# The end of a two-layer decoder on one core: grouped stores, one rare condition, four PSUM banks and spread row scaling

## The chip, the core and the metric

The kernel runs on one core of a Trainium2 chip. A core has five engines that run their own instruction streams: TensorE (PE, with its weight loads PEld), VectorE (DVE), ScalarE (ACT), GpSimd (POOL) and SyncE (SP, which mostly issues DMAs). They wait for each other on semaphores. The metric is the device time of one execution in microseconds (us), as the median of several runs; lower is better.

## The reference, cut to what matters

The reference is a decoder of two layers on x of 8 x 256 tokens with 256 features, in float32. Each layer adds self attention, cross attention to a context, and a feed-forward part, each on a layer norm of x. The change touches only the last part, the feed-forward of the second layer: a shared expert for every token, and one of eight routed experts for each token (top 1), weighted by a sigmoid gate.

```python
scores_aE = x_aD @ router_DE
vals_aK, idx_aK = jax.lax.top_k(scores_aE, K)                   # K = 1
masked_aE = jnp.full_like(scores_aE, -jnp.inf).at[jnp.arange(a)[:, None], idx_aK].set(vals_aK)
gates_Ea = jax.nn.sigmoid(masked_aE).T
routed_in_EaD = jax.lax.stop_gradient(gates_Ea[:, :, None] * x_aD[None, :, :])
mid_EaF = jax.nn.silu(jnp.einsum('ead,edf->eaf', routed_in_EaD, w1_eDF)) * jnp.einsum('ead,edf->eaf', routed_in_EaD, w3_eDF)
routed_out_EaD = jnp.einsum('eaf,efd->ead', mid_EaF, w2_eFD)
shared_aD = jax.nn.silu(x_aD @ ws1_DF) * (x_aD @ ws3_DF) @ ws2_FD
out_aD = shared_aD + routed_out_EaD.sum(axis=0)
...
x = x + _L1_ffn_ref(_layernorm(x, axis=-1), L1_ffn_router_DE, ...)
```

There are a = 2048 tokens, D = 256 features, F = 704 hidden features and 8 experts.

## The kernel before

Tokens are held as 16 tiles of 128 x 256 in `x`, on 128 partitions. All but the feed-forward part of the second layer is untouched by the change. That part is `token_experts`, and it has two kinds of work.

The shared expert works in four quarters of 512 tokens. `quarter(q)` makes the hidden values: six chunks of the 704 features (five of 128 and one of 64). For each chunk TensorE makes two products of 512 columns, h1 and h3 (L864; tiles `h1` and `h3` have two PSUM banks each), ScalarE takes silu of h1 into `sl` (L856), and VectorE multiplies `sl` by h3 into `mid` (L857). `joined(q, mid, i)` then makes the second product for one tile of 128 tokens (`out`, L1209, in a bank of the PSUM pool `emm`, which has two) and adds it to `x` on VectorE (L1220). The hidden values of quarters 0 and 1 are made before `token_experts` starts, under the names `hx` and `slx`.

The routed experts need tokens that are sorted by expert. VectorE works out each token's place `pos_i`. `gated(j)` scales the rows of token tile j: one product of the row's inverse deviation and its gate (L1234) and one normalisation into `xg` (L177). `put_rows(j)` scatters these rows on GpSimd's queue into `xs` in DRAM (an indirect DMA, L1294). Then `slots` works through 17 tiles of sorted rows. For each it reads the rows (GpSimd's queue, L1343; each read waits until all sixteen scatters have landed), reads an expert's weights (SyncE's queue, from `packs`; `w13` and `w2` have four buffers each), turns the rows on TensorE (`xrp`, L1370, in a bank of `emm`), makes the two products, and stores the result `ye` from ScalarE's queue. At the end sixteen indirect DMAs (L1446) gather each token's result back into `xg`.

The order of the stage is written by hand for TensorE and VectorE. It is: the second products of quarter 0 among the routing arithmetic, with the scaling of tiles 0 to 3 and their scatters; the scaling of tiles 4 to 15, each followed by its scatter on GpSimd; quarter 2; the second products of quarters 1 and 2; the 17 tiles; quarter 3; the gathers; and the last loop. In that loop VectorE adds four gathered tiles (L1456), each of them but 12 to 15 is stored by SyncE (L1458), then `joined(3, mid, i)` finishes tile 12 + i, which is stored too (L1460). These are sixteen stores of 128 KB each.

After the loop come two rare cases, which the inputs do not meet. Where the sorted tokens fill more than 17 tiles, the rest is worked off (`more`, a register load and a branch on every engine, L1464 and L1465). Where the first layer's routing was odd (`odd`, a load and a branch, L64 and L65), a whole second program `general` runs.

Of the kernel before, what the change touches and what calls it, by code (L numbers as in the profile page):

```python
# [28 lines left out]
F32 = mybir.dt.float32  # L29
BF16 = mybir.dt.bfloat16  # L30
I32 = mybir.dt.int32
U32 = mybir.dt.uint32
AF = mybir.ActivationFunctionType
ALU = mybir.AluOpType
# [4 lines left out]
P = 128  # L39
# [11 lines left out]
SLOTS = NT + E - 1  # L51
FIRST = 2 * FF
TILES = NT + E // 2
PAIRED = NT - E // 2
NEG = -1.0e30


@with_exitstack
def decoder(ctx: ExitStack, tc: tile.TileContext, a: dict, out: bass.AP):
    nc = tc.nc  # L60
    keep = ctx.enter_context(tc.tile_pool(name="keep", bufs=1))
    odd_i = keep.tile([P, 1], I32, name="odd_i")
    plain(tc, a, out, odd_i)
    odd = nc.values_load(odd_i[0:1, 0:1], min_val=0, max_val=1)  # L64
    with tc.If(odd > 0):  # L65
        general(tc, a, out)


@with_exitstack
def plain(ctx: ExitStack, tc: tile.TileContext, a: dict, out: bass.AP, odd_i: bass.AP):  # L70

    nc = tc.nc

    const = ctx.enter_context(tc.tile_pool(name="const", bufs=1))
    small = ctx.enter_context(tc.tile_pool(name="small", bufs=4))
    dram = ctx.enter_context(tc.tile_pool(name="dram", bufs=1, space=DRAM))

# [58 lines left out]

    dens = const.tile([P, 3, NT, H], F32, name="dens")

    xs = dram.tile([TILES * P, D], F32, name="xs")
    ye = dram.tile([TILES * P, D], F32, name="ys")

    yo = dram.tile([(TILES - 16) * P, D], F32, name="yo")

    packs = dram.tile([E, P, 2 * FIRST + NFC * D], F32, name="packs")

    def pack(e):

# [364 lines left out]
    def expert_tables():  # L514
        nc.sync.dma_start(gate, a["L0_ffn_gate_w"].rearrange("(c p) e -> p c e", p=P))
        nc.gpsimd.dma_start(experts, a["L0_ffn_experts"].rearrange("e (c p) f -> p e c f", p=P))
        zero = one.tile([P, D], F32, name="zero")
        nc.gpsimd.memset(zero, 0.0)
        nc.gpsimd.dma_start(xs.rearrange("(s p) d -> p s d", p=P), zero.unsqueeze(1).to_broadcast([P, TILES, D]))
        nc.gpsimd.dma_start(  # L520
            ye[17 * P :].rearrange("(s p) d -> p s d", p=P), zero.unsqueeze(1).to_broadcast([P, TILES - 17, D])
        )
        nc.gpsimd.dma_start(yo.rearrange("(s p) d -> p s d", p=P), zero.unsqueeze(1).to_broadcast([P, TILES - 16, D]))
        for e in range(E):
            nc.gpsimd.dma_start(packs[e, FF % P :, 2 * FIRST + FF // P * D :], zero[FF % P :])

        key_i = one.tile([P, E, TOP], I32, name="key_i")
        nc.gpsimd.iota(key_i, [[1, E], [E, TOP]], base=0, channel_multiplier=0)
        key = one.tile([P, S], F32, name="key")
        nc.vector.tensor_copy(key, key_i.rearrange("p e r -> p (e r)"))  # L530
        kps = mm.tile([P, 2, 2 * P], F32, tag="mm", name="kps")
        keycol = one.tile([P, 2], F32, name="keycol")
        for h in range(2):
            nc.tensor.transpose(kps[:, h, :P], key[:, bass.ts(h, P)], ident)
        nc.vector.tensor_copy(keycol, kps[:, :, 0])
        for h in range(2):
            nc.vector.tensor_scalar(later[:, h, :], key, keycol[:, h : h + 1], None, ALU.is_gt)
        num_i = one.tile([P, S], I32, name="num_i")
        nc.gpsimd.iota(num_i, [[1, S]], base=0, channel_multiplier=0)
        nc.vector.tensor_copy(num, num_i)  # L540
# [649 lines left out]
    def token_experts(phase):  # L1190
        one = phase.enter_context(tc.tile_pool(name="e1", bufs=1))
        work = phase.enter_context(tc.tile_pool(name="e2", bufs=2))
        wts = phase.enter_context(tc.tile_pool(name="e3", bufs=4))
        mm = phase.enter_context(tc.tile_pool(name="emm", bufs=2, space=PSUM))
        hp = phase.enter_context(tc.tile_pool(name="eh", bufs=2, space=PSUM))
        ws2, mid_s = shared["ws2"], shared["mid_s"]

# [34 lines left out]
        def gated(j):  # L1232
            (mv, rs), t = norms[j // 2], j % 2
            nc.vector.tensor_tensor(rs[:, t : t + 1], rs[:, t : t + 1], gates[:, j : j + 1], ALU.mult)  # L1234
            normed(xg[:, j, :], x[:, j, :], mv, rs, t)
# [51 lines left out]
        nc.vector.tensor_tensor(place, place, route["hot"], ALU.mult)  # L1287
        pos = one.tile([P, NT], F32, name="pos")
        nc.vector.tensor_reduce(pos, place, AX.X, ALU.add)
        pos_i = one.tile([P, NT], I32, name="pos_i")  # L1290
        nc.vector.tensor_scalar(pos_i, pos, TILES * P - 1.0, None, ALU.min)

        def put_rows(j):
# [25 lines left out]
        exp_f = one.tile([P, n_at], F32, name="exp_f")  # L1319
        nc.vector.tensor_reduce(exp_f, past.rearrange("p n k e -> p n (k e)"), AX.X, ALU.add)  # L1320
        nc.vector.tensor_scalar(tcol, tcol, filled[:, 0:1], None, ALU.is_ge)
        exp_i = one.tile([P, n_at], I32, name="exp_i")
        nc.vector.scalar_tensor_tensor(exp_i, tcol, 1.0 - E, exp_f, ALU.mult, ALU.add)
        gated(3)
        joined(0, mids[0], 3)
        put_rows(3)
        for j in range(4, NT):
            gated(j)
            put_rows(j)
        filled_i = one.tile([P, 1], I32, name="filled_i")  # L1330
        nc.vector.tensor_tensor(filled[:, 1:2], full_at[:, E:], all_at[:, E:], ALU.add)
        nc.vector.tensor_copy(filled_i, filled[:, 1:2])
        nc.vector.tensor_copy(odd_i, route["odd"])
        mids.append(quarter(2)[0])
        for i in range(4):
            joined(1, mids[1], i)
        for i in range(3):
# [50 lines left out]
        def outof(t, mid, sets):  # L1388
            ps = mm.tile([P, 2 * D], F32, tag="mm", name="out")[:, :D]
            for i in range(NFC):  # L1390
                for k, h in enumerate((slice(0, 64), slice(64, P))):
                    nc.tensor.matmul(  # L1392
                        ps[h],
                        mid[:, i, h],
                        sets[k % len(sets)][1][:, i, :],
                        start=i == 0,
                        stop=i == NFC - 1,
                        skip_group_check=True,
                    )
            yr = work.tile([P, D], F32, tag="yr", name="yr")  # L1400
            nc.scalar.copy(yr, ps)
            nc.scalar.dma_start(ye[bass.ts(t, P), :] if t < 17 else yo[bass.ts(t - 16, P), :], yr)

        def slots(order, beside=None):

            n = len(order)
            xr = [rows(t) for t in order[:2]]
            sets = [first_weights(order[0])]  # L1410
            if n > 1:
                sets.append(first_weights(order[1]))
            second_weights(sets[0])
            xrT = turned(xr)
            if beside:
                beside()
            xr = [rows(t) for t in order[2:4]]
            ahead = into(sets[0], xrT[0])
            for i, t in enumerate(order):
                now = ahead  # L1420
                if i + 2 < n:
                    sets.append(first_weights(order[i + 2]))
                if i + 1 < n:
                    second_weights(sets[i + 1])
                if i + 2 < n and i % 2 == 0:
                    xrT += turned(xr)
                    xr = [rows(t) for t in order[i + 4 : i + 6]]
                if i + 1 < n:
                    ahead = into(sets[i + 1], xrT[i + 1])
                outof(t, now, sets[i])  # L1430
# [14 lines left out]
        for j in places:  # L1445
# [4 lines left out]
                in_offset=bass.IndirectOffsetOnAxis(ap=pos_i[:, j : j + 1], axis=0),  # L1450
            )

        with tc.issue_after(last.ins), tc.manual_schedule(engines={mybir.EngineType.DVE}):
            for i in range(4):
                for j in places[4 * i : 4 * i + 4]:
                    nc.vector.tensor_tensor(x[:, j, :], x[:, j, :], xg[:, j, :], ALU.add)  # L1456
                    if j < 12:
                        nc.sync.dma_start(ov[j], x[:, j, :])  # L1458
                joined(3, mid, i)
                nc.sync.dma_start(ov[12 + i], x[:, 12 + i, :])  # L1460

        more = nc.values_load(filled_i[0:1, 0:1], min_val=2 * NT, max_val=2 * TILES - 1)  # L1464
        with tc.If(more > 34):  # L1465
            with tc.manual_schedule(engines={mybir.EngineType.PE}):
                slots([17])
                with tc.If(more > 36):
                    slots([18, 19])
            nc.vector.tensor_copy(pos, pos_i)  # L1470
            nc.vector.tensor_scalar(pos, pos, -16.0 * P, 0.0, ALU.add, ALU.max)
            beyond = one.tile([P, NT], I32, name="beyond")
            nc.vector.tensor_copy(beyond, pos)
            for j in range(NT):
                nc.gpsimd.indirect_dma_start(
                    out=xg[:, j, :],
                    out_offset=None,
                    in_=yo[:, :],
                    in_offset=bass.IndirectOffsetOnAxis(ap=beyond[:, j : j + 1], axis=0),
                )  # L1480
                nc.vector.tensor_tensor(x[:, j, :], x[:, j, :], xg[:, j, :], ALU.add)
                nc.sync.dma_start(ov[j], x[:, j, :])

    with ExitStack() as phase:
        token_experts(phase)
    w_s.close()


@with_exitstack
# [934 lines left out]
```

## Time and profile before

| what | value |
|---|---|
| median of three runs | 1406.7 us (1406.29 to 1408.69) |
| profiled execution | 1409.21 us |
| its span, first to last instruction | 1407.5 us |
| mean granted TensorE clock | 0.992 |
| TensorE busy | 1357.9 us, 96% of the span |
| VectorE, ScalarE, GpSimd busy | 36%, 32%, 28% |
| chain of work that ended last | PE 81%, DVE 6%, DMA 6% |

The profile shows one execution, so its times are summed against its own span; 1.7 us lie around the span. A row of the timeline gives the start, the length, the engine, the line of the kernel, the operation, the tile written and the tiles read, the shapes and how many instructions are taken together; in square brackets stands the idle time of the engine before it, and what ended it ("issue" means that the profile shows no releaser). PEclk is the clock that TensorE was granted, 1.00 for full speed. SPq, POOLq and so on are the engines' sequencers, which issue DMAs and take branches. Stage by stage, the last 240 us are: from 1171 to 1184 us second products and routing, from 1184 to 1206 us row scaling, scatters and quarter 2, to 1227 us second products, to about 1355 us the 17 tiles, then quarter 3 from 1363 us, and the last loop from 1382 us.

### The profile page before, as it was taken

Reading aid. Unit: us, or ns where it says so; the run is one execution under the profiler, and the core shown is the slowest. Engines: PE = TensorE matmul, PEld = TensorE weight load, DVE = VectorE, ACT = ScalarE, POOL = GpSimd, SP = SyncE. Lnnn points to the kernel's source line nnn. Section 1 sums busy time; section 2 is a strip of 40 time slices with the busy share of each in tenths; the row PEclk is TensorE's granted clock in tenths of the full one; section 3 lists DMA queues with packets and bytes.
Section 4 is the critical chain, followed back from the end, with each engine's and each line's share of the span. In section 5 each row is a group of like instructions: output and inputs, shape, how many; then the busy total and the mean of one; then the engine's idle time right before and its main releaser. Section 6 shows DMA issues by size and latency. Waiting matters only on the chain.

```text
span 1407.5 us, 28704 instructions
## 1 busy us (share of the span) xinstructions
PE 1357.9 (96%) x12198; PEld 884.4 (63%) x12198; DVE 502.7 (36%) x1465; ACT 456.8 (32%) x730; POOL 394.8 (28%) x499
## 2 busy tenths in 40 slices
PE   6999999999999999999999999999999999999995
PEld 3666756756766666665565656565565645788873
DVE  5443553653655744420122313221211336222212
ACT  2555444444444344422221313132221311122220
POOL 4232142142043244212141414233241523200013
PEclk9999999999999999999999999999999999999998
DMA  9950000000000006010101011010101013499943
GB/s 320 342 193 17 16 17 8 17 16 1 2 9 2 4 7 219 1 63 16 31 16 46 11 37 31 16 32 16 31 1 32 1 31 117 175 377 401 394 142 109
DMA packets 47069, 116.62 MB, mean 83 GB/s; under 512 B 8416, under 2 KB 30544, under 8 KB 42576
## 3 DMA queue, kind: packets, MB, share of 16 engines
q1 hardware_dynamic: 39056, 92.74, 19.3%
q0 software_dynamic: 5152, 18.89, 3.6%
q10 hardware_dynamic: 2720, 3.02, 0.6%
q8 instruction: 100, 1.64, 0.5%
q14 instruction: 41, 0.34, 0.1%
HBM read 104.00 MB, written 27.93 MB: 94 GB/s over the span
## 4 chain that ended last, share of the span: by engine, by line
PE 81%; DVE 6%; DMA 6%; POOL 3%; issue 2%; ACT 1%; SPq 1%; ACTq 0%; DVEq 0%; POOLq 0%
PE fm L191 12%; PE st L249 8%; PE o L281 8%; PE vps L191 8%; PE h L191 6%; PE wo L191 4%; PE ox L1055 4%; PE stx L1017 4%; PE out L1392 3%; PE qk L191 2%; PE hx L864 2%; PE tr L198 2%; PE out L1209 2%; PE h L864 2%; DMA packs<-L_ffn_w_eDF 2%; PE den L1031 2%
## 5 line engine op out<-in xcount | busy, mean ns | idle before, releaser
L281 PE MATMUL o<-pT,padv 128*64 128x256 f32 (+1 forms) x1536 | 171.6, 365 | 1.2 <-POOL pT L261 1.2
L258 ACT ACTIVATE pT<-st 128x1024 f32<-128x1024 f32 (+1 forms) x128 | 110.4, 915 | 88.3 <-PE st L249 87.5
L281 PEld LDWEIGHTS o<-pT,padv 128*64 128x64 f32 x1536 | 103.1, 137 | 53.0 <-issue 10.3
L249 PE MATMUL st<-qm,kT 64*128 64x256 f32 (+1 forms) x1024 | 116.2, 365 | 1.0 <-DVE qm L227 0.6
L191 PE MATMUL fm<-ctxT,wkv_x 128*64 128x256 f32 x1024 | 112.9, 380 | 0.0
L191 PE MATMUL vps<-wkv_x,ctxT 128*64 128x512 f32 x512 | 111.8, 593 | 0.0
L249 PEld LDWEIGHTS st<-qm,kT 64*128 64x128 f32 x1024 | 89.2, 188 | 25.9 <-issue 15.6
L191 PEld LDWEIGHTS fm<-ctxT,wkv_x 128*64 128x64 f32 x1024 | 73.1, 137 | 37.3 <-issue 1.3
L1023 POOL TENSOR_TENSOR both<-pTx 128x512 f32<-128x512 f32 x64 | 79.6, 1272 | 57.5 <-ACT pTx L1021 33.9
L1021 ACT ACTIVATE pTx<-stx 128x1024 f32<-128x1024 f32 x64 | 62.0, 1021 | 89.9 <-PE stx L1017 86.8
L191 PE MATMUL h<-xrT,w 128*64 128x128 f32 (+1 forms) x1936 | 86.9, 250 | 1.5 <-issue 1.5
L191 PEld LDWEIGHTS h<-xrT,w 128*64 128x64 f32 x1936 | 84.3, 137 | 4.4 <-issue 2.0
L191 PEld LDWEIGHTS vps<-wkv_x,ctxT 128*64 128x64 f32 x512 | 36.5, 137 | 68.9 <-issue 68.6
L258 ACT ACTIVATE pT<-st,kbias 128x1024 f32<-128x1024 f32 x64 | 68.0, 1113 | 28.8 <-PE st L249 28.7
L173 POOL TENSOR_TENSOR lnrs<-lnve,mhalf 128x2 f32<-128x2 f32 x48 | 34.2, 717 | 146.9 <-DVE lnve L171 93.7
L249 PE MATMUL st<-qm,memk 64*128 64x256 f32 x512 | 68.8, 393 | 0.5
L856 ACT ACTIVATE sl<-h 128x128 f32<-128x128 f32 (+1 forms) x114 | 35.3, 310 | 100.7 <-PE h L191 57.1
L1017 PE MATMUL stx<-qTx,kTx 64*128 64x256 f32 x512 | 64.3, 391 | 2.5 <-ACT pTx L1021 2.5
L857 DVE TENSOR_TENSOR midr<-sl,h 128x128 f32<-128x128 f32 x102 | 29.4, 288 | 101.5 <-PE h L191 69.7
L168 DVE BATCH_NORM_STATS2 lxst<-yx 128x6 f32<-128x256 f32 x16 | 6.0, 419 | 162.4 <-ACT yx L1115 162.4
L191 PE MATMUL qk<-l_wqkv,xnT 128*64 128x512 f32 x256 | 62.2, 608 | 0.7 <-ACT xnT L201 0.7
L261 POOL TENSOR_SCALAR_AFFINE_SELECT pT<-pT 128x512 f32<-128x512 f32 x64 | 39.5, 638 | 83.0 <-ACT pT L258 79.8
(272 smaller groups left out, 2082.5 us busy)
## 6 DMA issues: line engine op xcount, KB each, us to landing
w<-packs SPq DMA_DIRECT2D x22, 1408.0 KB
w<-packs SPq DMA_DIRECT2D x22, 768.0 KB
rs<-rd SPq DMA_DIRECT2D x16, 512.0 KB
packs<-L_ffn_w_eDF SPq DMA_DIRECT2D x8, 704.0 KB
packs<-L_ffn_w_eDF SPq DMA_DIRECT2D x8, 640.0 KB
packs<-L_ffn_w_eFD SPq DMA_DIRECT2D x8, 640.0 KB
ctxT<-ctx_T SPq DMA_DIRECT2D x8, 512.0 KB
wkv_x<-L_xattn_Wkv POOLq DMA_DIRECT2D x1, 4096.0 KB
```

The lines of the kernel that those rows point to most:

```text
L191: nc.tensor.matmul(out[h], lhsT[:, h], rhs, start=start, stop=stop, skip_group_check=True)
L249: nc.tensor.matmul(st[:, g, i, :n], kT[rows, c, bass.ts(kt, P)], qm[rows, 2 * mq + i, c, q0:], start=True, stop=True,)
L258: nc.scalar.activation(pT[:, :, :, :n], st[:, :, :, :n], AF.Exp, scale=scale, **kb)
L261: nc.gpsimd.affine_select(out=pT[:, :, :, :P], in_=pT[:, :, :, :P], compare_op=ALU.is_ge, fill=0.0, base=0, pattern=[[0, 2], [0, 2], [1, P ...
L281: nc.tensor.matmul(o[64 * i : 64 * i + 64, mq, q0:], v_pad[:, kt, 4 * c + 2 * mq + i, 2 * g : 2 * g + 2, :], pTs[kt][:, g, i, : S - q0], s ...
L856: nc.scalar.activation(sl, h1, AF.Silu)
L864: nc.tensor.matmul(h, shared["ws13"][:, c, lo : lo + P], shared["xnT"][:, c, bass.ts(q, 2 * S)], start=c == 0, stop=c == 1)
L1017: nc.tensor.matmul(st[:, g, kt, :], kT[rows, c, bass.ts(kt, P)], qT[rows, c, :], start=True, stop=True)
L1021: nc.scalar.activation(pT, st, AF.Exp, scale=scale)
L1023: nc.gpsimd.tensor_tensor(both, pT[:, :, 0, :], pT[:, :, 1, :], ALU.add)
L1055: nc.tensor.matmul(o[XD * g : XD * (g + 1), i, :], v[:, kt, 2 * (c2 + i) + g, :], pT[:, g, kt, :], start=kt == 0, stop=kt == 1, skip_group ...
L1392: nc.tensor.matmul(ps[h], mid[:, i, h], sets[k % len(sets)][1][:, i, :], start=i == 0, stop=i == NFC - 1, skip_group_check=True,)
```

## The change

There are four edits.

1. The last loop stores the four tiles of a group with one DMA of 512 KB where it stored each of them with its own. Tiles 12 to 15 are still stored singly. There are 7 stores instead of 16.
2. The two rare cases stand under one condition. VectorE works out `rare_i` (is the number of filled tiles above 17, plus `odd`) before quarter 2, and one load and one branch on it follow the last stores. The code for more than 17 tiles becomes a function `beyond` of its own. For this `pos_i`, `exp_i`, `filled_i` and `rare_i` move to the outermost SBUF pool, and the DRAM tensors `xs`, `packs` and `yo` to an outer DRAM pool.
3. The PSUM pool `emm` has four banks instead of two.
4. The scaling and scattering of tiles 4 to 15 is written two tiles at a time after each of the six chunks of quarter 2.

```diff
+COMMON = NT + 1
...
-    odd_i = keep.tile([P, 1], I32, name="odd_i")
-    plain(tc, a, out, odd_i)
-    odd = nc.values_load(odd_i[0:1, 0:1], min_val=0, max_val=1)
-    with tc.If(odd > 0):
-        general(tc, a, out)
+    dram = ctx.enter_context(tc.tile_pool(name="dram", bufs=1, space=DRAM))
+    odd_i, filled_i, rare_i = (keep.tile([P, 1], I32, name=n) for n in ("odd_i", "filled_i", "rare_i"))
+    pos_i = keep.tile([P, NT], I32, name="pos_i")
+    exp_i = keep.tile([P, PAIRED + 2 * (TILES - PAIRED)], I32, name="exp_i")
+    xs = dram.tile([TILES * P, D], F32, name="xs")
+    packs = dram.tile([E, P, 2 * FIRST + NFC * D], F32, name="packs")
+    yo = dram.tile([(TILES - COMMON + 1) * P, D], F32, name="yo")
+    stored = plain(tc, a, out, dram, odd_i, filled_i, rare_i, pos_i, exp_i, xs, packs, yo)
+    rare = nc.values_load(rare_i[0:1, 0:1], min_val=0, max_val=2)
+    with tc.If(rare > 0):
+        filled = nc.values_load(filled_i[0:1, 0:1], min_val=2 * NT, max_val=2 * TILES - 1)
+        with tc.If(filled > 2 * COMMON):
+            beyond(tc, out, pos_i, exp_i, xs, packs, yo, stored)
+        odd = nc.values_load(odd_i[0:1, 0:1], min_val=0, max_val=1)
+        with tc.If(odd > 0):
+            general(tc, a, out)
...
-        mm = phase.enter_context(tc.tile_pool(name="emm", bufs=2, space=PSUM))
+        mm = phase.enter_context(tc.tile_pool(name="emm", bufs=4, space=PSUM))
...
-        for j in range(4, NT):
-            gated(j)
-            put_rows(j)
-        filled_i = one.tile([P, 1], I32, name="filled_i")
         nc.vector.tensor_tensor(filled[:, 1:2], full_at[:, E:], all_at[:, E:], ALU.add)
         nc.vector.tensor_copy(filled_i, filled[:, 1:2])
         nc.vector.tensor_copy(odd_i, route["odd"])
-        mids.append(quarter(2)[0])
+        nc.vector.tensor_scalar(filled[:, 1:2], filled[:, 1:2], 2 * COMMON + 0.5, None, ALU.is_gt)
+        nc.vector.tensor_tensor(rare_i, filled[:, 1:2], route["odd"], ALU.add)
+        mids.append(mid_s[0])
+        for i, _ in enumerate(hidden_shared(2, pair, silu)):
+            for j in (2 * i + 4, 2 * i + 5):
+                gated(j)
+                put_rows(j)
...
+        stored = []
         with tc.issue_after(last.ins), tc.manual_schedule(engines={mybir.EngineType.DVE}):
             for i in range(4):
-                for j in places[4 * i : 4 * i + 4]:
+                group = places[4 * i : 4 * i + 4]
+                for j in group:
                     nc.vector.tensor_tensor(x[:, j, :], x[:, j, :], xg[:, j, :], ALU.add)
-                    if j < 12:
-                        nc.sync.dma_start(ov[j], x[:, j, :])
+                if i:
+                    lo = group[0]
+                    stored.append(nc.sync.dma_start(ov[lo : lo + 4].rearrange("t p d -> p t d"), x[:, lo : lo + 4, :]))
                 joined(3, mid, i)
-                nc.sync.dma_start(ov[12 + i], x[:, 12 + i, :])
-        more = nc.values_load(filled_i[0:1, 0:1], min_val=2 * NT, max_val=2 * TILES - 1)
-        with tc.If(more > 34):
...
+                stored.append(nc.sync.dma_start(ov[12 + i], x[:, 12 + i, :]))
+        return stored
```

## The prediction

> **What bounds the kernel now.** I read the page first (busy shares, chain), then the windows of the last 250 us, then TensorE's timeline there, then every engine's timeline from 1380 us on, and last SyncE's waits and branches.
>
> ```profile
> PE 1357.9 (96%) x12198; PEld 884.4 (63%) x12198; DVE 502.7 (36%) x1465; ACT 456.8 (32%) x730; POOL 394.8 (28%) x499
> ...
> PE 81%; DVE 6%; DMA 6%; POOL 3%; issue 2%; ACT 1%; SPq 1%; ACTq 0%; DVEq 0%; POOLq 0%
> ```
>
> TensorE (PE) is the bound over the whole span; the edits can only pay where it has a hole, or after its last product. The windows show both places.
>
> ```profile
> 1188.00:1192.00 4.00, 2.69 (x7) 0.90 (x5) 3.78 (x13) 0.00 (x0) 3.09 (x4) 1.00 0.98 380
> 1192.00:1196.00 4.00, 2.38 (x3) 1.17 (x4) 2.09 (x8) 0.60 (x1) 2.89 (x4) 0.65 1.00 404
> ...
> 1224.00:1340.00 116.00, 113.79 (x2031) 99.23 (x2030) 25.47 (x88) 32.78 (x108) 6.92 (x13) 1.00 0.93 366
> ...
> 1380.00:1400.00 20.00, 12.83 (x54) 9.69 (x52) 8.27 (x22) 0.59 (x1) 5.42 (x5) 0.95 0.44 137
> 1400.00:1407.50 7.50, 0.00 (x0) 0.00 (x0) 0.00 (x0) 0.00 (x0) 0.00 (x0) 0.50 0.13 41
> ```
>
> The columns are length, busy time of PE, PEld, DVE, ACT, POOL, then granted clock, DMA share, GB/s. At 1188 to 1196 PE is busy 5.07 of 8 us, with the clock at 0.65 in the second half, while DVE is nearly full. From 1400 on no engine computes for 7.5 us.
>
> ```profile
> 1170.99 8.02 PE L1209 MATMUL out<-ws,mid 128*128 128x256 f32 x36
> 1179.25 2.86 PE L1209 MATMUL out<-ws,mid 128*128 128x256 f32 x12 [0.24 <-DVE x L1220]
> 1181.94 8.75 PE L864 MATMUL h<-xnTe,ws 128*128 128x512 f32 x20
> 1193.62 12.05 PE L864 MATMUL h<-xnTe,ws 128*128 128x512 f32 x24 [2.93 <-issue]
> 1205.51 18.29 PE L1209 MATMUL out<-ws,mid 128*128 128x256 f32 x84
> ```
>
> The third and fourth rows are quarter 2. It stops after two and a half chunks for 2.93 us, and its other 24 products take 12.05 us where 24 steps of 0.429 us make 10.3. "issue" hides the releaser: the next product overwrites an h3 bank that DVE's first product L857 has yet to read, and that one stands in DVE's order behind all the row scaling:
>
> ```profile
> 1192.04 0.14 DVE L1234 TENSOR_TENSOR rstd<-rstd,gates 128x1 f32<-128x1 f32 x1
> 1192.22 0.44 DVE L177 TENSOR_SCALAR xg<-x,mean,rstd 128x256 f32<-128x256 f32 x1
> ...
> 1192.89 1.27 DVE L857 TENSOR_TENSOR mid<-sl,h 128x512 f32<-128x512 f32 x2
> ```
>
> The end, by start and length:
>
> ```profile
> 1388.74 0.42 DVE L1220 TENSOR_TENSOR x<-x,out 128x256 f32<-128x256 f32 x1 [3.84 <-PE out L1209]
> ...
> 1389.21 5.45 PE L1209 MATMUL out<-ws,mid 128*128 128x256 f32 x24 [1.83 <-DVE x L1220]
> ...
> 1394.70 0.42 DVE L1220 TENSOR_TENSOR x<-x,out 128x256 f32<-128x256 f32 x1 [0.83 <-PE out L1209]
> ...
> 1396.00 3.87 SPq L1458 DMA_DIRECT2D out<-x  x4
> 1399.96 0.38 SPq L1460 DMA_DIRECT2D out<-x  x1
> ```
>
> DVE is done at 1395.12, but SyncE is still issuing stores, the last until 1400.34. Then it takes the branch of the first rare case at 1400.39, waits for the landings to 1402.40, and takes the second branch:
>
> ```profile
> SPq L65 <- SPq L65: 2.7, 1, 2.7
> ```
>
> That is SyncE from its branch L65 at 1402.47 to its next instruction at 1405.21; 2.27 us more close the program.
>
> **The change part by part.** The profiled execution took 1409.21 us, with a span of 1407.5; the median shown is 1406.7, 2.5 lower. I sum on the profile's axis and take the saving off the median.
>
> *Row scaling between the chunks.* Twelve pairs (0.15 + 0.44 or 0.62 us, about 0.65 with gaps) leave DVE's stretch before the first product of quarter 2; two pairs follow each of its six chunks. A chunk lasts 8 x 0.429 = 3.43 us on PE and now 0.69 + 1.3 = 2.0 on DVE, so DVE keeps pace and each h3 bank is read over 1 us before PE needs it. The stall goes: -2.93. So do the slow products after it: 12.05 - 10.3 = -1.74. That the second belongs to the first is a reading of the granted clock, 0.5 for 3.4 us from 1193.2. [...] Quarter 3, the same 44 products without a hole, takes 19.1 us, against 23.57 here.
>
> The twelve scatters (POOL, 0.96 us every 1.26) move with the scaling. In before they ran to 1202.1; now each pair waits for its chunk, and the last ends near 1205.7. Behind them in POOL's queue stand the reads of the sorted rows, which wait for all sixteen landings: issued at 1208.9, 6.8 us after the last scatter. Now 1212.5, data some 2 to 3 us later. PE wants them for xrp at 1223.64 - 4.3 = 1219.3: slack about 4 us, cost nothing. SyncE's prefetch of weights keeps its order; of two register loads among it one is left, whose value is ready earlier than before.
>
> *Four banks.* Taken away: the 0.24 us wait of the fourth output of quarter 0, and 1.83 us at 1389.2. Added: the first output of quarter 0 now takes a bank that quarter 1's last products used, so it waits for their L857 on DVE, which ended at 1171.91, where PE could start at 1170.99. Nothing is queued on PE but the outputs and quarter 2. Sum before quarter 2: 0.9 of delay, part of it given back by the wait removed: +0.47 (fourth output ends 1182.3 for 1181.84).
>
> PE so far: 0.47 - 2.93 - 1.74 = -4.2. The routed tiles follow: their weight loads are released as PE frees buffers, so they shift with it. The DMA engines are nearly full there (0.93 at 366 GB/s), PE waits 1.46 us at 1246.3 and 0.68 at 1296.5. These could go or double: 2.1 us either way; I take them as unchanged.
>
> *The end*, in the old coordinates. With four banks the four outputs run from 1382.04 without a wait, 48 x 0.2158 = 10.4, to 1392.4. The unexplained part is DVE's pause: its add L1220 came at 1388.74 though its output was ready by about 1384.9. If the pause recurs, three groups of four adds and one (0.34 + 1.34 each) bring the last add to 1393.8 to 1394.2; if not, PE sets it at 1392.5 to 1392.9. I take the recurring one: PE had no part in the pause, and nothing here removes its code.
>
> *Stores.* Sixteen issues become seven. The single ones cost 0.35 to 0.40, at times 1 us; the 512 KB form (128x4x256) is in the trace as the ctxT loads of L977, 0.37 to 0.51, none longer. The last store of four is issued near 1393.9, the last single ends at 1394.6 to 1394.9, against 1400.34. A price: the last four tiles leave together, so 512 KB instead of 128 start late. At the 250 GB/s of 1390 to 1394 they move in 2.1 us and land about 2 later, at 1397.7; the single store of before landed 2.06 after its issue.
>
> *One condition.* One load and one branch go from each engine, and two small DVE operations (0.15 each) come in before quarter 2's first product, which has over 0.5 us to spare. On SyncE the first branch was cheap: its wait events follow 0.2 us after. The second was dear: 2.74 us to the next instruction, after the landings. The one left jumps over both rare parts, so it is a far one; but nothing makes it wait for the landings, it follows the stores: 1394.9 + 2.75 = 1397.65, beside the landings instead of after them. [...] The rows show 2.7 on SyncE and 3.98 for PE's record, so I use those. PE's branch starts at 1392.4 and ends at 1396.4, DVE's (2.9) at 1397.1, both in time. Then 2.27 to close: 1397.7 + 2.27 = 1399.9, against 1407.48: -7.6. Without DVE's pause -8.8.
>
> Sum: -4.2 - 7.6 = -11.8. The span becomes 1395.7, the median 1406.7 - 11.8 = 1394.9.
>
> **The rivals.**
>
> *The stores' landing or another engine sets the end.* For it: twice as much data leaves in the last microseconds as in before, and POOL's two internal updates of 1.5 us each run late. Against: POOL drained at 1401.4 after two branches and now has one. If the last landing comes at 1402, the end keeps only the order of branch and landing: -3.2, in all -7.4, 1399.3.
>
> *PE's hole stays in another form.* Products L857 came late in before even without scaling ahead of them (one waited 6.1 us for "remote", while SyncE's and POOL's queues were full). If that recurs on a product PE waits for, the 4.7 stay: -7.1, 1399.6. The same size follows if the scatters come late: rows landing after 1219.3 cost their lateness plus the slow clock.
>
> *Better than forecast.* No pause on DVE (-1.2) and no PE waits among the tiles (-2.1): 1391.6.
>
> *Slower than before: the weight stream.* The change moves xs, packs and yo to other pools and shifts SBUF addresses. The tiles need about 40 MB between 1226 and 1347, 335 GB/s, and have some 400 at full share. If the moved placement lowered the rate, PE would wait for w13 and w2 from 335 on; 305 would make 40 / 0.305 = 131 us for 121, cost 11 and eat the gain; at 290 the time is 1411. Against: the access pattern and sizes are the same.
>
> *The change does not do what it says* cannot fully be: the instruction orders of both programs show the scatters between the chunks and seven stores.
>
> **How the numbers follow.** Forecast 0.55; end kept by landings 0.13; PE's hole kept 0.13; better 0.12; weight stream 0.05; both gains small 0.02. What a measurement can tell is 0.2%, 2.8 us. The range reaches from the better case, 1391.0, to just over the two one-sided cases, 1400.5, leaving about 0.15 out. Faster 0.94, same 0.02, slower 0.04.
>
> **What would show it.** Right: no gap over 0.3 us in quarter 2's 44 products, granted clock 1.0 at 1185 to 1205, about 19 us long; a wait near 0.9 on the first output of quarter 0; xrp with no idle before it; four outputs of quarter 3 back to back; the last store issued within 0.8 us of the last DVE add; SyncE's 2.7 us beside the landings. Wrong: a PE wait before xrp or in quarter 2, tiles longer than 121 us, stores of four taking over 1 us to issue, or a landing more than 4 us after the last add.

## The result and the profile after

The changed kernel takes 1396.55 us in the median (1395.14 to 1397.70), the kernel before 1406.49 us on the same chip; the ratio is 0.9927 with a 95% interval of 0.9909 to 0.9944. That is 9.9 us less by the medians and 10.3 by the ratio (7.9 to 12.8 by the interval), where 11.8 were forecast; the time lies inside the range. The profiled execution took 1396.5 us with a span of 1394.8.

First the page of the changed kernel, its busy times and the chain that ended last:

```profile
PE 1357.5 (97%) x12198; PEld 884.4 (63%) x12198; DVE 502.4 (36%) x1467; ACT 457.4 (33%) x730; POOL 395.7 (28%) x499
...
PE 85%; DVE 5%; POOL 4%; issue 1%; ACT 1%; DMA 0%; ACTq 0%; POOLq 0%; DVEq 0%; SPq 0%
```

TensorE has the same work and a larger share of a shorter span; DMA has left the chain. The windows that answer to the two holes of before (columns as before: length, busy PE, PEld, DVE, ACT, POOL, clock, DMA share, GB/s):

```profile
1188.00:1192.00 4.00, 4.00 (x10) 1.71 (x9) 2.18 (x8) 0.60 (x1) 2.46 (x3) 1.00 0.98 345
1192.00:1196.00 4.00, 4.00 (x11) 1.80 (x10) 2.18 (x8) 0.60 (x1) 2.10 (x3) 1.00 1.00 413
...
1376.00:1394.80 18.80, 12.42 (x53) 9.69 (x51) 8.43 (x22) 0.59 (x1) 5.48 (x5) 0.95 0.50 158
```

PE is busy all of 1188 to 1196 at full clock, and DVE has fallen from nearly full to about half. PE's timeline shows the same place by products (the lines have moved: L1292 is the second product, L947 the first product of the shared expert, L1303 the add of its output, L1541 and L1543 the stores):

```profile
1173.42 10.63 PE L1292 MATMUL out<-ws,mid 128*128 128x256 f32 x48 [0.84 <-DVE mid L940]
1183.89 19.05 PE L947 MATMUL h<-xnTe,ws 128*128 128x512 f32 x44
1202.77 18.29 PE L1292 MATMUL out<-ws,mid 128*128 128x256 f32 x84
```

Quarter 2 is one row of 44 products. The new wait of 0.84 us stands ahead of quarter 0's outputs, as forecast. The end, from the timeline of all engines, and SyncE's wait behind its one branch:

```profile
1377.90 10.52 PE L1292 MATMUL out<-ws,mid 128*128 128x256 f32 x48
...
1387.66 0.54 SPq L1541 DMA_DIRECT2D out<-x  x1
1388.46 0.42 DVE L1303 TENSOR_TENSOR x<-x,out 128x256 f32<-128x256 f32 x1 [0.83 <-PE out L1292]
1388.91 0.33 SPq L1543 DMA_DIRECT2D out<-x  x1
```

```profile
SPq L77 <- SPq L77: 3.1, 1, 3.1
```

The last add ends at 1388.88, the last store is issued at 1389.24, SyncE branches at 1389.29 and goes on at 1392.47. The last store has landed at 1392.72, ahead of the last of SyncE's nine waits behind the branch (1393.07). The two profiles differ by 12.7 us, and this is where, each length from one event to the next:

| stretch | before | after | difference |
|---|---|---|---|
| start to the same product of quarter 1 (not touched by the change) | 1161.05 | 1162.51 | +1.46 |
| to the first output of quarter 0 | 9.94 | 10.91 | +0.97 |
| quarter 0's outputs | 10.95 | 10.47 | -0.48 |
| quarter 2 | 23.57 | 18.88 | -4.69 |
| to the first output of quarter 3 | 176.53 | 175.13 | -1.40 |
| to the end of the last add | 13.08 | 10.98 | -2.10 |
| to the end of the last store's issue | 5.22 | 0.36 | -4.86 |
| to SyncE's next instruction after the far branch | 4.87 | 3.23 | -1.64 |
| to the end | 2.27 | 2.31 | +0.04 |

The first row is not the change's, and the profiled execution of before was 2.7 us over its median, that of after was at its median. So the table shows more than the medians moved, and the experiments had to say which rows belong to the kernel.

### The profile page after: what moved, and what is told of

Same layout as the page of the kernel before. It is cut to its first block, busy times and chain, and to the rows that moved or that the text cites. A ratio compares the mean times of both kernels' runs of the same rounds, so it can differ in the third digit from the quotient of the medians.

```text
span 1394.8 us, 28640 instructions
## 1 busy us (share of the span) xinstructions
PE 1357.5 (97%) x12198; PEld 884.4 (63%) x12198; DVE 502.4 (36%) x1467; ACT 457.4 (33%) x730; POOL 395.7 (28%) x499
## 4 chain that ended last, share of the span: by engine, by line
PE 85%; DVE 5%; POOL 4%; issue 1%; ACT 1%; DMA 0%; ACTq 0%; POOLq 0%; DVEq 0%; SPq 0%
PE fm L274 12%; PE st L332 9%; PE o L364 9%; PE vps L274 8%; PE h L274 6%; PE wo L274 4%; PE ox L1138 4%; PE stx L1100 4%; PE out L1475 3%; PE out L1292 3%; PE h L947 3%; PE qk L274 3%; PE hx L947 3%; PE tr L281 3%; PE den L1114 2%; PE ao L274 2%
```

## The experiments

All are timed against the kernel before on their chip. Ratios, with 95% intervals, and the same in us of 1406.5:

| kernel | ratio | us |
|---|---|---|
| changed kernel | 0.9927 (0.9909 to 0.9944) | -10.3 |
| before + spread scaling | 0.9970 (0.9960 to 0.9979) | -4.2 |
| before + four banks | 0.9996 (0.9986 to 1.0006) | -0.6 |
| before + grouped stores | 0.9997 (0.9986 to 1.0009) | -0.4 |
| before + one condition | 0.9973 (0.9963 to 0.9983) | -3.8 |
| changed, single stores | 0.9945 (0.9931 to 0.9959) | -7.7 |
| changed, two conditions | 0.9963 (0.9949 to 0.9978) | -5.2 |
| changed, three banks | 0.9922 (0.9907 to 0.9936) | -11.0 |
| changed, ten scalings ahead | 0.9941 (0.9921 to 0.9961) | -8.3 |
| changed, no branch | 0.9908 (0.9887 to 0.9930) | -12.9 |
| changed, three banks, last store by ScalarE | 0.9916 (0.9896 to 0.9937) | -11.8 |

### Each edit alone

**The scaling spread over quarter 2, alone.**

```diff
-        for j in range(4, NT):
-            gated(j)
-            put_rows(j)
...
-        mids.append(quarter(2)[0])
+        mids.append(mid_s[0])
+        for i, _ in enumerate(hidden_shared(2, pair, silu)):
+            for j in (2 * i + 4, 2 * i + 5):
+                gated(j)
+                put_rows(j)
```

> The kernel before with the row scaling alone spread over quarter 2's chunks. My theory: quarter 2's 44 products run without a hole in about 18.9 us (23.6 before), granted clock 1.0, the rows' reads near 1212 are early enough, and nothing else moves: 4.7 us less, median near 1401.8. Rival (the hole moves): PE waits at xrp or in quarter 2 for a late product of VectorE, and the gain is under 2 us.

Median 1402.32. PE's timeline of this kernel, with the whole quarter in one row:

```profile
1183.45 19.05 PE L864 MATMUL h<-xnTe,ws 128*128 128x512 f32 x44
```

The 4.2 us (3.0 to 5.6 by the interval) fit the hole and the slow clock behind it, 4.7 together. The hole did not move elsewhere: from quarter 2's end to quarter 3's first product it is 158.1 us, 157.5 in before.

**Four banks, alone.**

```diff
-        mm = phase.enter_context(tc.tile_pool(name="emm", bufs=2, space=PSUM))
+        mm = phase.enter_context(tc.tile_pool(name="emm", bufs=4, space=PSUM))
```

> The kernel before with four banks alone. My theory: the first output of quarter 0 waits 0.8 to 1.0 us for VectorE, quarter 2 keeps its hole, the four outputs of quarter 3 run without a wait; at the end SyncE's sixteen issues still set the time, so the outputs' earlier end is worth less than 1 us: in all between -1 and +0.7, no measurable change. Rival: the banks are what shortens the end, 2 us or more less.

Median 1406.55, no change that can be told. PE's timeline shows the new wait, and quarter 2's hole, which stays:

```profile
1176.35 10.63 PE L1209 MATMUL out<-ws,mid 128*128 128x256 f32 x48 [0.84 <-DVE mid L857]
...
1198.03 12.26 PE L864 MATMUL h<-xnTe,ws 128*128 128x512 f32 x24 [2.46 <-DVE mid L857]
```

Here the trace names the releaser that the profile of before called "issue": L857, the product in VectorE's queue behind the scaling.

**Grouped stores, alone.**

```diff
-                for j in places[4 * i : 4 * i + 4]:
+                group = places[4 * i : 4 * i + 4]
+                for j in group:
                     nc.vector.tensor_tensor(x[:, j, :], x[:, j, :], xg[:, j, :], ALU.add)
-                    if j < 12:
-                        nc.sync.dma_start(ov[j], x[:, j, :])
+                if i:
+                    lo = group[0]
+                    nc.sync.dma_start(ov[lo : lo + 4].rearrange("t p d -> p t d"), x[:, lo : lo + 4, :])
```

> The kernel before with the stores of four tiles alone. My theory: the last issue follows the last VectorE add within 0.8 us (5.2 before), the two branches and the landing stay in their order: landing about 2 us after the last issue, then 2.7 us for the far branch: 4 to 5 us less, median near 1402. Rival: the 512 KB that leave late land later than that, 4 us or more after the last issue, and the gain is 2 us or less.

Median 1406.68: my theory failed, and so did its rival. The issue does follow the last add at once, and the landings are not late (SyncE has seen the last of them at 1397.24, 2.4 us after the issue ended). The timeline, then SyncE's waits (in all, times, longest):

```profile
1393.94 0.42 DVE L1220 TENSOR_TENSOR x<-x,out 128x256 f32<-128x256 f32 x1 [0.83 <-PE out L1209]
1394.38 0.49 SPq L1462 DMA_DIRECT2D out<-x  x1
```

```profile
SPq L65 <- SPq L65: 3.7, 1, 3.7
SPq L2422 <- PEq L2422: 2.9, 2, 2.4
```

The second row is new: SyncE is ready to close at 1402.47 and then waits 2.4 us at the program's closing barrier (L2422). PE is named there, but its own last instruction before the barrier ended at 1401.0, so it had been done before SyncE was; the late one is GpSimd. Its rows, by line (minimum, median, maximum in ns, then the start of the first and of the last):

```profile
L65 POOLq COMPARE_BRANCH  x1: 45/45/45, 1393.4 to 1393.4; - x1
...
L65 POOLq INC_SWDGE_SEM  x1: 1470/1470/1470, 1397.8 to 1397.8; - x1
```

```profile
L2422 POOLq DRAIN  x3: 46/109/5382, 1399.3 to 1405.2; - x3
```

After the second branch GpSimd is away for 3.9 us (1393.4 to 1397.4), then updates its DMA semaphores for 1.47, and drains for 5.38: 1399.29 + 5.38 = 1404.67. So once SyncE is faster, GpSimd's own chain of two branches ends the program. Even without this edit the two run close: in the profiles of the spread scaling alone and of four banks alone, which keep the end of before, GpSimd's drain ends 0.3 and 0.5 us after SyncE is ready (1399.49 for 1399.16, and 1407.25 for 1406.78).

**One condition, alone.** The function for more than 17 tiles and the moved tensors are those of the change; the rest is as before.

```diff
-    odd = nc.values_load(odd_i[0:1, 0:1], min_val=0, max_val=1)
-    with tc.If(odd > 0):
-        general(tc, a, out)
+    rare = nc.values_load(rare_i[0:1, 0:1], min_val=0, max_val=2)
+    with tc.If(rare > 0):
+        ...
```

> The kernel before with the one condition alone (and the tensors that move out for it). My theory: the sixteen stores end as before, SyncE's one far branch of about 2.7 to 3.2 us runs beside the landings instead of after them: about 2 us less, median near 1404.5. Rival: the one branch costs what both did, no gain; a rival on the other side: the moved tensors slow the weights' stream, and the 17 tiles take more than 121 us.

Median 1403.56; by the ratios 3.8 us less (2.4 to 5.2), where about 2 were expected. The end of its timeline and SyncE's wait behind the branch:

```profile
1396.26 0.42 DVE L1303 TENSOR_TENSOR x<-x,out 128x256 f32<-128x256 f32 x1 [0.83 <-PE out L1292]
...
1396.84 3.28 SPq L1538 DMA_DIRECT2D out<-x  x4
1400.21 0.38 SPq L1540 DMA_DIRECT2D out<-x  x1
```

```profile
SPq L77 <- SPq L77: 2.8, 1, 2.8
```

SyncE branches at 1400.65 without waiting for the landings. GpSimd has drained by 1399.94. Now the stores are what is late: 3.9 us after the last add. (This execution, at 1407.61 us, was the slowest of the kernel's 22, so the size of that is not its usual one.) From quarter 2's end to quarter 3's first product it is 157.1 us, 157.5 in before, so the moved tensors show no cost.

### The pause of before, looked at once more

> The kernel before, profiled once more. My theory: VectorE's pause of 3.84 us before the first add of quarter 3's outputs belongs to that one execution, not to the kernel: the four outputs take 10.5 to 11 us from the first product, and from there to the end of the program it is 21 to 22 us (25.5 before). Rival: the pause is the kernel's own and recurs at the same add, and the change took it away.

The same program, profiled again, took 1408.22 us (span 1406.5). VectorE's and SyncE's timelines and SyncE's waits:

```profile
1387.26 0.42 DVE L1220 TENSOR_TENSOR x<-x,out 128x256 f32<-128x256 f32 x1
...
1394.94 0.42 DVE L1220 TENSOR_TENSOR x<-x,out 128x256 f32<-128x256 f32 x1 [0.83 <-PE out L1209]
```

```profile
1393.22 3.62 SPq L1458 DMA_DIRECT2D out<-x  x4
1396.94 0.38 SPq L1460 DMA_DIRECT2D out<-x  x1
```

```profile
SPq L1465 <- SPq L1465: 3.7, 4, 2.9
SPq L65 <- SPq L65: 2.6, 1, 2.6
```

There is no pause. The last store's issue ends 1.96 us after the last add, not 5.22. From the first output of quarter 3 to the end it is 22.1 us; in the first profile it was 25.4, and in the changed kernel 16.9. In this execution SyncE is ready to close at 1405.66 and GpSimd at 1404.31. So grouped stores could gain at most those 1.35 us here, in keeping with the -0.4 that they measured. The 5.22 us on which the forecast took the stores' lateness are the largest of all: the profiles with sixteen single stores end their last issue 5.2, 2.0, 1.5, 1.1, 3.9 and 1.3 us after the last add (before twice, spread scaling, four banks, one condition, and the changed kernel with single stores below).

The theory is half right. The pause is not a fixture of the kernel, but it is no freak of one execution either. Of the thirteen profiles of this study four have it, always between the fourth gathered tile's add and the first output's: the first of before (4.26 us from start to start) and the three kernels at the end of this section, which were all run on one chip (4.06 to 4.20). The other nine have 0.44 there. On that chip the kernel before took 1409.74 in the median, 2.0 to 3.3 us more than on the others. Those three kernels have three or four banks, so PE does not stop behind the pause, and from the first output to the start of the last add it is 11.5 to 11.7 us (10.6 without a pause); in before, with two banks, it was 12.7.

What holds VectorE there is a signal of PE, as the row's releaser says (3.84 <-PE out). The add waits for a semaphore that PE raises. In the changed kernel, which has no pause, the trace has four such signals 1.5, 1.9, 2.3 and 2.8 us after the first product of the outputs, and the add starts 0.1 us behind the fourth. In the four with a pause the last three or four come in a burst, at most 0.13 us from first to last (1388.59 to 1388.71 in before), 6.5 to 6.7 us after that product, while PE's rows run on. So the forecast's "PE had no part in the pause" was wrong: the products were not late, PE's signals were. Why they were late stays open; it does not follow the edits.

### Each end edit taken back from the changed kernel

**Single stores again** (the grouped store's diff turned round).

> The changed kernel with sixteen single stores again, all else as changed. My theory: with one condition left SyncE's chain alone sets the end, so single stores show in full: the last issue 1.5 to 4 us after the last add instead of 0.4, 1.5 to 3.5 us slower than the changed kernel, median 1398 to 1400. Rival: as in the kernel before they are worth nothing, median within 1 us of the changed kernel.

Median 1399.57; by the ratios 2.6 us slower than the changed kernel (-7.7 for -10.3), the intervals overlap a little. SyncE's timeline:

```profile
1389.25 2.93 SPq L1539 DMA_DIRECT2D out<-x  x4
1392.27 0.43 SPq L1541 DMA_DIRECT2D out<-x  x1
```

The last add ended at 1391.39 and the last issue at 1392.70, 1.3 us later, where it is 0.36 in the changed kernel. So with one condition the stores seem to be worth something, as the theory had it, though the lateness is below its 1.5 to 4 us. The 2.6 us are not secured: from the last add to the end of the program the two traces differ by 0.5 us only (6.4 and 5.9), and the rest of their difference lies ahead of it.

**Two conditions again** (the kernel before with the other three edits, their diffs as above).

> The changed kernel with the two rare cases under their own conditions again (the kernel before with the other three edits). My theory: the end is set by GpSimd, which closes after two branches, two updates of 1.5 us and a drain of 5.4 us, so the grouped stores are lost on it: 4 to 5 us slower than the changed kernel, median near 1401, and the last store still within 0.8 us of the last add. Rival: SyncE's two branches in a row set it, with the same sum but the drain of GpSimd ending over 1 us before SyncE's last wait.

Median 1402.16, by the ratios 5.1 us slower than the changed kernel. GpSimd's drain and SyncE's wait for it:

```profile
L2423 POOLq DRAIN  x3: 46/109/5382, 1394.3 to 1400.3; - x3
```

```profile
SPq L2423 <- PEq L2423: 2.8, 2, 2.3
```

SyncE is ready at 1397.63, GpSimd drained at 1394.31 + 5.38 = 1399.70. So the theory holds, and its rival (GpSimd done over 1 us before SyncE) does not. With two conditions the drain begins 14.8 us after quarter 3's first output; in the changed kernel it is 8.3, and it ends at 1391.57, well ahead of SyncE's 1393.94:

```profile
L2483 POOLq DRAIN  x3: 46/109/5382, 1386.2 to 1394.5; - x3
```

So by the ratios the grouped stores are worth 0.4 us or nothing with two conditions and some 2.6 with one; and the one condition is worth 3.8 us with single stores and 5.1 with grouped ones. That each is worth more beside the other is not shown, since the intervals of these differences overlap. They cut two chains that end side by side, SyncE's and GpSimd's.

### The new bank wait, and the clock behind a hole

**Three banks.**

```diff
-        mm = phase.enter_context(tc.tile_pool(name="emm", bufs=4, space=PSUM))
+        mm = phase.enter_context(tc.tile_pool(name="emm", bufs=3, space=PSUM))
```

> The changed kernel with three banks in place of four. My theory: three banks do not reach the bank that quarter 1's last products used, so the first output of quarter 0 starts without its wait of 0.84 us, and at the end the outputs still run without one: 0.5 to 1 us less, median near 1395.8, not to be told from the changed kernel by its median. Rival: three are too few beside VectorE's adds at the end, and it is 1 us slower.

Median 1396.42. PE's timeline shows the outputs of quarter 0 without their wait, and those of quarter 3 have none either:

```profile
1172.01 8.23 PE L1292 MATMUL out<-ws,mid 128*128 128x256 f32 x37
...
1377.20 10.52 PE L1292 MATMUL out<-ws,mid 128*128 128x256 f32 x48
```

The trace agrees with the theory; 0.7 us by the ratios is too little to be told from the changed kernel.

**Ten scalings ahead of quarter 2.**

```diff
         mids.append(mid_s[0])
+        for j in range(4, 14):
+            gated(j)
+            put_rows(j)
         for i, _ in enumerate(hidden_shared(2, pair, silu)):
-            for j in (2 * i + 4, 2 * i + 5):
+            for j in range(2 * i + 14, min(2 * i + 16, NT)):
```

> The changed kernel with ten of the twelve scalings again ahead of quarter 2 and the last two after its first chunk. My theory: the hole in quarter 2 comes back, shorter by two scalings, 1.5 to 2.3 us; if a hole of that size still lowers the granted clock, quarter 2 takes 22 to 24 us and the kernel is 3.5 to 5 us slower than the changed one (median near 1400.5)[...].

Median 1402.45 against 1409.74 for before on that chip: 2.0 us slower than the changed kernel by the ratios, with intervals that overlap, so the trace has to decide. PE's timeline, and the window around the hole:

```profile
1195.75 10.57 PE L947 MATMUL h<-xnTe,ws 128*128 128x512 f32 x24 [1.60 <-DVE mid L940]
```

```profile
1190.00:1197.00 7.00, 5.40 (x13) 2.20 (x12) 6.64 (x23) 1.19 (x2) 5.22 (x6) 1.00 0.96 380
```

The hole of 1.60 us left the granted clock at 1.00, and the 24 products behind it take 10.57. Quarter 2 is 20.75 us from its first product to the next stage's, 1.87 over 18.88. (Its end is longer for another reason: one store of four took 2.1 us to issue.) In the profiles with holes of 2.46 to 3.27 the clock fell every time, and the 24 products took 11.98 to 13.48. So only the hole is lost with this short one, while the longer ones lost clock as well.

The length of a hole alone does not decide, though. In each profile the granted clock fell only on a grid of 3.413 us: in before at 19.04, 305.76 and 1193.23 us, 84 and 260 periods apart. Cut along that grid (columns as before), first the hole of before and the period behind it, then another gap of before, 2.59 us long from 198.28 us on, which an edge of the grid divides:

```profile
1189.82:1193.23 3.41, 0.87 (x3) 0.04 (x1) 3.23 (x13) 0.00 (x0) 2.80 (x3) 1.00 0.98 405
1193.23:1196.64 3.41, 3.02 (x4) 1.47 (x5) 0.93 (x2) 0.60 (x1) 2.50 (x4) 0.50 0.99 399
...
196.53:199.95 3.42, 1.75 (x16) 1.10 (x12) 2.13 (x6) 2.21 (x3) 3.42 (x4) 1.00 0.21 66
199.95:203.36 3.41, 2.49 (x38) 1.73 (x38) 1.51 (x3) 1.27 (x2) 0.14 (x1) 1.00 0.04 13
```

And the hole of this run:

```profile
1191.98:1195.39 3.41, 2.17 (x6) 0.62 (x4) 3.26 (x10) 0.00 (x0) 2.50 (x4) 1.00 0.97 383
1195.39:1198.80 3.41, 3.05 (x7) 1.44 (x8) 2.73 (x7) 0.60 (x1) 2.80 (x3) 1.00 1.02 405
```

The hole of before left PE idle for 2.54 us of one period, and the next was granted half the clock; here it was 1.24 us, and in the divided gap 1.67 at most, and the clock stayed. In all thirteen profiles, from 25 us after the start to 12 us before the end, every one of the 28 periods in which PE idled for 2.12 us or more was followed by a fall. Of all the others, which reach up to 1.99 us, one was (1.36 us idle at 618 us, four banks alone). So a hole like that of before cost clock here when 2.12 us or more of it fell into one period; in the five profiles that have it, it did.

### Two tries at the last microseconds

**No branch.**

```diff
     with tc.If(rare > 0):
-        filled = nc.values_load(filled_i[0:1, 0:1], ...)
-        with tc.If(filled > 2 * COMMON):
-            beyond(...)
-        odd = ...
-        with tc.If(odd > 0):
-            general(tc, a, out)
+        nc.vector.tensor_copy(odd_i, filled_i)
```

> The changed kernel with the bodies of both rare cases left out: under the condition stands one small VectorE copy, so the branch is taken over a few instructions. For these inputs neither body runs. My theory: the branch costs its length because its target is far; near it, SyncE's next instruction follows within 0.5 us instead of 3.17, then the landings of the last stores set the end, 1 to 2 us less, median near 1395. Rival: the branch itself costs it, SyncE still pauses 2.5 us or more and nothing is gained.

The built program has no branch left at all, presumably because nothing uses the copy's result, so the near branch was not tried; what ran is the end without any. Median 1396.52 where before took 1409.74; 2.6 us less than the changed kernel by the ratios, with intervals that overlap. SyncE's last store and its waits:

```profile
1389.98 0.52 SPq L1538 DMA_DIRECT2D out<-x  x1
```

```profile
SPq L2478 <- DMA out<-x: 2.1, 3, 1.4
```

SyncE now waits for the landings, the last of which it has seen at 1393.26, 2.8 us after the issue ended. From the end of the last add to the end of the program it is 4.6 us; with the branch it was 5.9. So beside the landings a far branch of 3.2 us costs about 1.3, in keeping with the forecast's "beside the landings instead of after them". From 1360 us on the two DMA queues that the profile calls "instruction" move 11 packets in the changed kernel and one in this one; whether the 3.2 us have to do with them is not shown.

**Three banks, and ScalarE issues the last store.**

```diff
-                stored.append(nc.sync.dma_start(ov[12 + i], x[:, 12 + i, :]))
+                by = nc.scalar if i == 3 else nc.sync
+                stored.append(by.dma_start(ov[12 + i], x[:, 12 + i, :]))
```

> The changed kernel with three banks, and the very last store issued by ScalarE instead of SyncE. My theory: SyncE branches 0.7 us earlier beside ScalarE's store, VectorE's chain (add, load, branch) becomes the last to close: 1 to 2 us less than the changed kernel, median near 1395. Rival: ScalarE's own load and far branch come after its store and end as late as SyncE's did, no gain over three banks alone.

Median 1398.34, on the chip where before took 1409.74; its ratio cannot be told from that of three banks alone. From the end of the last add to the end of the program it is 7.2 us, more than the 5.9 of the changed kernel, so the rival is right: the gain is lost to the branches. SyncE's waits:

```profile
SPq L77 <- SPq L77: 4.5, 1, 4.5
```

SyncE branches at 1389.37 and ScalarE at 1390.27, and both are away until 1393.9 to 1394.0. Why they took 4.5 and 3.7 us, longer than SyncE's 3.17 in the changed kernel, is not shown. No version here is shown to beat the changed kernel.

## Why the prediction was right, point by point

- *The hole in quarter 2 and its clock, -2.93 - 1.74.* Right: -4.69 in the profile, 4.2 us alone, so the clock went with the hole, as the forecast read it from the row. The rows along the grid, with ten scalings ahead, show when a hole cost clock as well: 2.12 us of idle time in one period of 3.413 us were enough, and the hole of before had 2.54 in one.
- *Scatters late, no cost.* Right: the last was issued at 1206.71 and the reads of the sorted rows at 1211.91, and xrp at 1220.90 has no idle time before it.
- *The new bank wait, +0.47.* Right: 0.97 later, 0.48 given back.
- *The tiles unchanged.* Nearly: 1.40 us less between quarter 2 and quarter 3's outputs, of which 0.68 is a PE wait that this execution lacks. It is one of the waits that come and go: none, or 0.2 to 0.95 us, near the same product in the other profiles. Over all thirteen the whole stretch takes 175.1 to 177.1 us.
- *VectorE's pause recurs.* Wrong for this execution: the profile after does not have it. It comes and goes (four profiles of thirteen) and is neither the change's nor removed by it. And it is a late signal of PE, which the forecast had ruled out.
- *The end, -7.6.* The mechanism was right and the term mis-sized. In its own terms (profile against profile) it was -8.56, close to the -8.8 given for no pause. But 3.3 us of the end of that first profile (25.4 for 22.1 us) were that execution's own, 2.1 of them the pause, in an execution 2.7 us over the median that the saving was taken from. Against the second profile the end is worth 16.9 - 22.1 = -5.2. With -4.2 for PE that makes -9.4, and the medians show -9.9. As far as 11.8 was too large (it lies inside the interval of 7.9 to 12.8), this is the term.
- *Stores from 1400.34 to 1394.6.* As a saving of its own it fails: alone it is worth 0.4 us. The text saw that GpSimd has "two branches and now has one", but not how close GpSimd ends to SyncE in the kernel before (1.35 us ahead in the second profile, though 5.3 in the first, the one that was read). The sum held, since the same change shortens GpSimd's chain too (its drain begins 8.3 us after quarter 3's first output, 14.8 with two conditions); that the two edits came together was luck for this term.
- *The far branch, 2.74.* Right in kind, 3.17 in the changed kernel, 2.5 to 4.5 in all. The branch's own record on SyncE is 45 to 53 ns; the time is lost behind it.

Of the rivals, another engine setting the end is what happens as soon as the two conditions stay (grouped stores alone, and the changed kernel with two conditions); the hole in another form, late rows and a slower weight stream did not occur.

## What to carry to other kernels

Before a saving is summed against one profiled execution, profile the kernel a second time and take only what both show; a pause that the trace does not explain may not be there in the next execution (four profiles of thirteen had this one). At the end of this program each engine took a branch of its own, and GpSimd drained for 5.38 us behind it, so ask for each one when it is done: an edit that shortened one engine's end gained only up to the next one's (grouped stores alone, 0.4 us or nothing). A product that waits behind a queue of small work on another engine can be freed by moving that work between the chunks of its own stage: here the same twelve scalings cost nothing there (the 44 products took 18.88 us from the first to the next stage's, 23.57 before). And ask of a hole on TensorE not only how long it is but how much of it falls into one period of the grid of 3.413 us on which the granted clock fell here.

## What the runs showed of the hardware that was not expected

- The granted clock fell on a grid of 3.413 us, after a period in which PE idled for 2.12 us or more (28 of 28 periods in thirteen profiles), and not, but for one case, after one with 1.99 us or less.
- VectorE's pause of about 4 us (4.06 to 4.26 from one add to the next) at one and the same instruction, in all three profiles of one chip and none of the eight on two others. It waits for PE's signals, which the trace has in a burst 3.7 to 3.9 us late; why they are late is open.
- GpSimd's closing drain took 5.382 us in before, in the changed kernel, with grouped stores alone and with two conditions again, and each condition added 1.47 to 1.50 us for an update of its DMA semaphores, beside its branch.
- A far branch held SyncE for 2.5 to 4.5 us across these kernels, while a near one (the first condition's, in the kernels with two) let it go on in about 0.2 to 0.5. That the distance is the cause is not shown: PE's record of that near branch was 4.02 us in before and 4.76 in the kernel with grouped stores alone, as long as of a far one.
- The issue of a store, single or of four tiles, mostly took 0.33 to 0.55 us on SyncE, but single ones of before took 1.1 to 1.7 three times in its last loop, and one of four tiles 2.1 (ten scalings ahead).
